# Attention over 16 heads: in every fourth step the row exponentials are kept, turned in 32x32 blocks and multiplied with V in 32x32 tiles

## The chip, the cores and the metric

The kernel runs on one core of one Trainium2 chip. The metric is the time of one execution on the device, in microseconds (us); the median of several runs is compared. All work is in fp32, save the row maxima, which are split into bf16 parts.

## The reference

```python
Q = split_heads(x @ Wq.T + bq); K = split_heads(x @ Wk.T + bk); V = split_heads(x @ Wv.T + bv)
tQ = split_heads(tokens @ Wq.T + bq); tK = split_heads(tokens @ Wk.T + bk)
cQ = Q + tQ;  cK = K + tK
scores = einsum('bhqd,bhkd->bhqk', cQ, cK) / sqrt(32)
out = einsum('bhqk,bhkd->bhqd', softmax(scores), V)
return x + merge_heads(out)
```

Here x is 8 batches of 512 rows and 512 features, there are 16 heads of 32 features, and tokens is one condition vector of 512 features for each batch.

## The kernel before

A **step** t is one batch and four heads (128 features), so there are 32 steps, four to a batch. One core does everything; the program's order on each engine is written out by hand, and PSUM's eight banks are dealt out by a table of turns, `TURNS`, read through `banks(i)`: in each item of a step four banks take scores and four take row scores, and banks that are free again take projections or results.

Each step has four **items**, and in each of them TensorE does the following for other steps than its own as well.

- `exponentials(t, kc)`: the scores of step t **a second time**, keys on the partitions and all 512 queries along the free axis. First a bf16 product with ones (L597) puts the negative row maximum into the bank, then the fp32 product of K and Q (L600) adds the scores. ScalarE (ACT) makes the exponential into a tile `e` (L611).
- `row_max(t+1, qc)`: the scores of the next step, queries on the partitions (`row_scores`, L526). VectorE (DVE) takes the negative maximum over the keys (L494 for one head, L535 for two).
- `denominators(t+1, qc)`: ACT makes the exponential of these row scores with the maximum as its bias (L545). Before, only the sum over the keys is kept (`accum_out`); the exponentials go to a tile `dead` that nobody reads.
- In three items a quarter of the projections of the next batch (q, k, v), done by a scheme of seven block products (`product`, L407): `first_products` and `other_products` in turn, each with additions on DVE (L432, L442, L451, L452, L465, L466).
- In one item (the second) `weighted(t-1)`: 16 products of V with the exponentials (`times_v`, L616), a small product that spreads the sums (`spread_sums`, L647), and `send`: DVE turns the result in 32x32 blocks (L672), POOL multiplies with the reciprocal and adds x and the bias (L673, L674), SP stores it.

Between these, `split_max` (POOL, L559 to L562) and `turn_max` (a transposing DMA on SP's queue) bring the row maxima of the next step into the form that L597 needs; `turn_x` (DVE, L323) turns the next batch's x; `combine_x` (DVE, L333 to L337) makes block sums of it; `load_residual` loads x for the residual and POOL adds the bias (L173).

An fp32 matmul of the code runs as two weight loads and two matmuls, and the profile counts each of them: 512 calls of L526 are 1,024 records.

Of the kernel before, what the change touches and what calls it, by code (L numbers as in the profile page):

```python
# [9 lines left out]
F32 = mybir.dt.float32  # L10
# [7 lines left out]
def kernel(  # L18
# [38 lines left out]
    nc = tc.nc  # L57
# [11 lines left out]
    HS = S // 2  # L69

    const = ctx.enter_context(tc.tile_pool(name="const", bufs=1))
    stage = ctx.enter_context(tc.tile_pool(name="stage", bufs=3))
    xp = ctx.enter_context(tc.tile_pool(name="xp", bufs=4))
    xtp = ctx.enter_context(tc.tile_pool(name="xtp", bufs=2))
    qkp = ctx.enter_context(tc.tile_pool(name="qkp", bufs=3))
    ep = ctx.enter_context(tc.tile_pool(name="ep", bufs=13))
    op = ctx.enter_context(tc.tile_pool(name="op", bufs=2))
# [31 lines left out]
    ]  # L109
    turn = [0]  # L110

    def banks(i, n=1):

        j = TURNS[turn[0]][i]
        if n == 1:
            return psum[:, j, :]
        k = TURNS[turn[0]][i + 1]
        return psum[:, j : k + 1 : k - j, :]

    def advance():  # L120
        turn[0] = {7: 0, len(TURNS) - 1: 4}.get(turn[0], turn[0] + 1)

# [9 lines left out]
    def load_x(n, queue=nc.sync):  # L132

        if n < B * NS:
            xs[n] = xp.tile([P, D], F32, tag="x", name=f"x_{n}")
            queue.dma_start(xs[n], x[n // NS, n % NS * P : (n % NS + 1) * P, :])
# [15 lines left out]

    xr = {}

    def turned_by_vector(t):
# [3 lines left out]
    def load_residual(t):  # L159

        b, g = divmod(t, G)
        if turned_by_vector(t):
            xr[t] = op.tile([P, NB, BL], F32, tag="xr", name=f"xr_{t}", bufs=3)
            for h in range(HG):
                nc.sync.dma_start(
                    xr[t][h * BL : (h + 1) * BL], spread(x[b], g * P + h * BL)
                )
            bias = bvs[:, g, :].unsqueeze(1).broadcast_to([P, NB, BL])
        else:

            xr[t] = xT[b][:, g, :]
            bias = bvl.broadcast_to([P, S])
        nc.gpsimd.tensor_tensor(xr[t], xr[t], bias, ALU.add)  # L173

    ws = {}
    for n in ("q", "k", "v"):
# [21 lines left out]
    load_x(1)  # L198
    wk0 = op.tile([P, D], F32, tag="dead", name="wk0")
    nc.scalar.dma_start(wk0, Wk[:P, :])  # L200

    cond_sb = const.tile([B + 2, D], F32, tag="cond", name="cond_sb")
    nc.sync.dma_start(cond_sb[:B, :], cond)
# [31 lines left out]
    make_identity(nc, ident)  # L235
    split = []
    for i in range(2):
        m = const.tile([P, NS, HG, HD], BF16, tag=f"split{i}", name=f"split{i}")
        nc.vector.memset(m, 0.0)
        split.append(m)  # L240

# [61 lines left out]
    def transpose_x(n, pt, leaves=nc.vector.tensor_copy):  # L303
# [10 lines left out]
        leaves(xT[b][:, :, sc * P : (sc + 1) * P], pt.rearrange("p (c s) -> p c s", c=NC))  # L314
        load_block(n + NC)

    def turn_x(n):
        b, cc = divmod(n, NC)
        if b >= B:
            return  # L320
        if cc == 0:
            xT[b] = xtp.tile([P, NC, S], F32, tag="xT", name=f"xT_{b}")
        nc.vector.transpose(xT[b][:, cc, :], xs[n].rearrange("p f i -> p (f i)"))  # L323
        load_block(n + NC)

# [108 lines left out]
    def first_products(n, b, u, dens, small, at, first=0, held=None):  # L434
# [18 lines left out]
        plus(n, b, u, 1, c22, one_[:, HS:], c12)  # L453

    def other_products(n, b, u, dens, small, at):

# [40 lines left out]

    def row_max(t, qc, hold=False):

# [3 lines left out]
        for j in range(HG):  # L503
            row_scores(t, qc, j, banks(HG + j))
        if t < T - 2 or t * NS + qc == T * NS - 1:
            for j in range(2):
                one_max(t, qc, j, banks(HG + j))
        else:
            row_max_of(t, qc, 0, banks(HG, 2))
        last, both = [banks(HG + 2), banks(HG + 3)], banks(HG + 2, 2)  # L510

        def held():
            if hold and t < T - 2:
                for j in range(2):
                    one_max(t, qc, 2 + j, last[j])
            else:
                row_max_of(t, qc, 1, both)
# [20 lines left out]

    def denominators(t, qc, prs=range(NP)):

        if t >= T - 2:
            return
        for j in [pr * 2 + i for pr in prs for i in range(2)]:
            dead = op.tile([P, S], F32, tag="dead", name=f"dead_{t}_{qc}_{j}")
            nc.scalar.activation(  # L545
                dead,
                banks(HG + j),
                AF.Exp,
# [4 lines left out]
    def split_max(t, on=nc.gpsimd):  # L553

        if t >= T:
            return
# [9 lines left out]
    def turn_max(t):  # L566

        if t >= T:
            return
# [22 lines left out]
    def exponentials(t, kc, at=None):  # L592

        bank = [psum[:, i, :] for i in at] if at else [banks(i) for i in range(HG)]
        for j in range(HG):
# [28 lines left out]
    def times_ones(of, pt, start, stop):  # L624
        for j in range(HG):
# [6 lines left out]
            )  # L632

    def masked(t):

        apart = op.tile([P, HG, NS, NS], F32, tag="apart", name=f"apart_{t}")
        nc.gpsimd.tensor_tensor(
# [7 lines left out]
    def spread_sums(apart, pd):  # L645
        for h in range(HG):
# [6 lines left out]
            )  # L653

    def weighted(t, pt, pd, between):

# [3 lines left out]
        for kc in range(NS):  # L660
            times_v(t, kc, pt)
            if kc == 0:
                spread_sums(apart, pd)
        rec = op.tile([P, NB, 1], F32, tag="recs", name=f"recs_{t}")
        nc.vector.reciprocal(rec, pd[:, :NB].unsqueeze(2))
        between()
        send(t, pt, rec)

    def send(t, y_, rec):

        y = op.tile([P, NB, BL], F32, tag="res", name=f"res_{t}")
        nc.vector.transpose(y.rearrange("p f e -> p (f e)"), y_)  # L672
        nc.gpsimd.tensor_tensor(y, y, rec.broadcast_to([P, NB, BL]), ALU.mult)  # L673
# [16 lines left out]
    def condition(n, pt):  # L690


        for cc in range(NC):
            nc.tensor.matmul(pt[cc * HD : (cc + 1) * HD, :], condT[:, cc, :], wT[n][:, cc, :])  # L694
        part[n] = const.tile([P, D], F32, tag=f"part{n}", name=f"part_{n}")
        nc.scalar.copy(part[n], pt)
# [18 lines left out]
    for _ in range(28):  # L715
        nc.tensor.matmul(warm[:, :P], onesb, onesb, start=True, stop=True)
    def bank(i):
        return psum[:, i, :]

# [84 lines left out]
    parts = {}  # L804

    def part_of(t, pt, of, between=None):

# [4 lines left out]
        if t in parts:  # L812
            p = op.tile([P, S], F32, tag="dead", name=f"part_{t}_{of[0]}")
            nc.scalar.copy(p, pt)
# [17 lines left out]

    for t in range(T - 3):
        b, r = divmod(t, G)

        exponentials(t, 0)
        held = row_max(t + 1, 1, r % 2)
        of = ((t - 1) // G + 1, (t - 1) % G)
        dens = lambda: denominators(t + 1, 1)
        if t:  # L840
            project_pair("q", *of, dens, nothing, 1 if r % 2 else (0, 3), held)
        else:
            first_products("v", 0, 0, dens, nothing, 1)
            turn_x(NC + 2)
            load_residual(1)
        turn_x(t + NC + 3)
        advance()

        exponentials(t, 1)
        row_max(t + 1, 2)  # L850
        dens = lambda: denominators(t + 1, 2)
        if t:
            dens()
            weighted(
                t - 1, banks(0), banks(1), lambda: combine_x(b + 1, r) if r < 2 else None
            )
        else:
            dens()
            other_products("v", 0, 0, nothing, nothing, (0, 2))
        advance()  # L860

        exponentials(t, 2)
        rest = row_max(t + 1, 3, r % 2)

        def held():
            rest()
            split_max(t + 1)
            turn_max(t + 1)

        dens = lambda: denominators(t + 1, 3)  # L870
        if t:
            project_pair("k", *of, dens, nothing, 1 if r % 2 else (0, 3), held)
        else:
            held()
            first_products("v", 0, 1, dens, nothing, 1)
            combine_x(1, 0)
        if t:
            load_residual(t + 1)
        advance()

        exponentials(t, 3)
        held = row_max(t + 2, 0, r % 2)
        dens = lambda: denominators(t + 2, 0)
        project_pair("v", *of, dens, nothing, 1 if r % 2 else (0, 2), held)
        advance()


# [15 lines left out]
    def crossed(t, kc, qc, u=None):  # L903
# [37 lines left out]
        row_max_of(u, qc, 1, banks(HG + 2, 2))  # L941

    t = T - 3
    row(4)
# [59 lines left out]
    sum_of(t, acc2, 2, nc.vector)  # L1004
    den = op.tile([P, NB, BL], F32, tag="dead", name=f"den_{t - 1}")
    nc.vector.transpose(den.rearrange("p f e -> p (f e)"), pd)
# [21 lines left out]

    part_x = op.tile([P, S], F32, tag="dead", name="part_x")
    nc.vector.tensor_tensor(part_x, pd, xr[t], ALU.mult)  # L1030
    den = op.tile([P, S], F32, tag="dead", name="den")
    nc.scalar.copy(den, pd)
    store_30(nc.scalar, (2,))
    oT = op.tile([P, S], F32, tag="res_last", name="oT", bufs=1)
    y = op.tile([P, NS, P], F32, tag="xr_last", name="res", bufs=1)
    rec = op.tile([P, NS, HG, 1], F32, tag="rec", name="rec")
# [57 lines left out]
```

## Time and profile before

| | |
|---|---|
| median of 3 runs (lowest, highest) | 715.58 us (715.08, 716.7) |
| the profiled execution: its time, its span | 717.11 us, 715.0 us |
| granted TensorE clock, mean | 0.998 |
| POOL busy | 176.5 us |
| second scores' exponentials, L611 on ACT | 488 of 603 ns |
| row exponentials, L545 on ACT | 480 of 706 ns, and 225 ns to read each sum |
| a transpose of 128x512 on DVE, L323 | 28 of 701 ns |
| a reduce of 128x512, of 128x1024 on DVE, L494 and L535 | 324 of 685 ns, 88 of 1,215 ns |

The span is the time from the first to the last instruction that the profiler records; the run's own time is some 2 us longer. "Busy" is the union of an engine's recorded instructions; a mean duration can be longer than the distance between two starts, since instructions of an engine overlap. TensorE's matmul ends are modelled. PE is TensorE's matmuls, PEld its weight loads.

### The profile page before, as it was taken

The numbers are of one execution on the slowest core, as the hardware profiler recorded it, in microseconds if no ns is written. First come the engines' busy times: TensorE is split into PE (matmuls) and PEld (weight loads), VectorE is DVE, ScalarE is ACT, GpSimd is POOL, SyncE is SP. The second block draws the span as 40 slices with busy tenths as digits, with TensorE's granted clock in tenths as the row PEclk, the third lists the DMA queues.
The fourth block names the chain that finished last, engine by engine and source line by source line (L and its number), as shares of the span: only waits on it lengthen the run. The fifth ranks groups of instructions, "written<-read, shape, count | busy, mean of one in ns | idle before, by whom it ended". The sixth has DMA issues, their size and how long they took to land.

```text
span 715.0 us, 22748 instructions
## 1 busy us (share of the span) xinstructions
PE 705.7 (99%) x9160; PEld 321.1 (45%) x9160; DVE 535.3 (75%) x918; ACT 604.7 (85%) x1497; POOL 176.5 (25%) x275
## 2 busy tenths in 40 slices
PE   8999999999999999999999999999999999999996
PEld 7445444444444444444444444444444444444431
DVE  4798767877768877778777877777777777667776
ACT  2589888888889899898888889899898898889674
POOL 3712221122221122221122221122221122221451
PEclk9999999999999999999999999999999999999999
DMA  7634321323322323321323321322211222311111
GB/s 181 106 61 68 54 40 29 53 42 51 53 33 41 51 42 50 54 42 32 50 42 52 53 40 32 51 43 49 39 28 17 35 39 39 39 30 19 31 31 30
DMA packets 223390, 33.43 MB, mean 47 GB/s; under 512 B 221610, under 2 KB 222122, under 8 KB 223284
## 3 DMA queue, kind: packets, MB, share of 16 engines
q1 hardware_dynamic: 221524, 30.92, 26.4%
q8 instruction: 72, 1.18, 0.7%
q10 hardware_dynamic: 1760, 1.05, 0.5%
q14 instruction: 34, 0.28, 0.1%
HBM read 19.75 MB, written 8.39 MB: 39 GB/s over the span
## 4 chain that ended last, share of the span: by engine, by line
PE 93%; DVE 2%; DMA 2%; issue 1%; ACT 1%; POOL 0%; SPq 0%; DVEq 0%; POOLq 0%
PE psum L407 39%; PE psum L526 16%; PE psum L616 15%; PE psum L600 14%; PE psum L597 5%; PE psum L350 2%; DMA maxT<-split 1%; DVE acc L894 1%; PE psum L920 1%; DMA w_q<-in_L_cond_Wq_dram 1%; PE psum L266 0%; DVE nmax L535 0%; DVE acc L892 0%; PE psum L694 0%; PE psum L311 0%
## 5 line engine op out<-in xcount | busy, mean ns | idle before, releaser
L545 ACT ACTIVATE dead<-psum,nmax 128x512 f32<-128x512 f32 x480 | 327.4, 706 | 5.6 <-DVE nmax L494 3.1
L611 ACT ACTIVATE e<-psum 128x512 f32<-128x512 f32 x488 | 252.0, 603 | 69.5 <-PE psum L600 69.3
L494 DVE TENSOR_REDUCE nmax<-psum 128x1 f32<-128x512 f32 x324 | 208.3, 685 | 133.4 <-PE psum L526 133.4
L526 PE MATMUL psum<-kT,qT 32*128 32x512 f32 x1024 | 141.1, 598 | 0.0
L673 POOL TENSOR_TENSOR res<-res,recs 128x512 f32<-128x512 f32 x30 | 31.4, 1047 | 419.9 <-DVE res L672 419.9
L600 PE MATMUL psum<-qT,kT 32*128 32x512 f32 x976 | 125.5, 587 | 0.0
L616 PE MATMUL psum<-e,v 128*32 128x512 f32 x1024 | 121.2, 596 | 0.0
L535 DVE TENSOR_REDUCE nmax<-psum 128x2 f32<-128x1024 f32 x88 | 106.8, 1215 | 2.7 <-PE psum L526 2.7
L545 ACT ACTIVATION_READ_ACCUMULATOR dead<-psum,nmax 128x1 f32 x480 | 107.8, 225 | 0.0
L526 PEld LDWEIGHTS psum<-kT,qT 32*128 32x128 f32 x1024 | 59.5, 182 | 55.9 <-ACT dead L545 16.9
L616 PEld LDWEIGHTS psum<-e,v 128*32 128x32 f32 x1024 | 26.6, 110 | 65.1 <-issue 37.6
L407 PE MATMUL psum<-wc_v,xc 128*32 128x256 f32 x768 | 50.2, 379 | 0.0
L600 PEld LDWEIGHTS psum<-qT,kT 32*128 32x128 f32 x976 | 48.6, 185 | 2.2
L597 PE MATMUL psum<-maxT,onesb 3*128 3x512 bf16 x488 | 48.1, 385 | 1.2 <-DMA maxT<-split 1.1
L407 PE MATMUL psum<-xc,wc_k 128*32 128x256 f32 x720 | 47.1, 379 | 0.0
L407 PE MATMUL psum<-xc,wc_q 128*32 128x256 f32 x720 | 47.1, 379 | 0.0
L173 POOL TENSOR_TENSOR xr<-xr,bvs 128x512 f32<-128x512 f32 x31 | 39.4, 1270 | 20.5 <-DMA x<-in_x_dram 13.1
L597 PEld LDWEIGHTS <-onesb 3*128 3x128 bf16 x488 | 12.3, 91 | 65.7 <-issue 60.2
L674 POOL TENSOR_TENSOR res<-res,xr 128x512 f32<-128x512 f32 x30 | 38.6, 1286 | 2.3
L407 PE MATMUL psum<-wT_v,xT 128*32 128x256 f32 x512 | 36.8, 382 | 0.0
L407 PE MATMUL psum<-xT,wT_k 128*32 128x256 f32 x480 | 34.5, 382 | 0.0
L407 PE MATMUL psum<-xT,wT_q 128*32 128x256 f32 x480 | 34.5, 382 | 0.0
(168 smaller groups left out, 710.0 us busy)
## 6 DMA issues: line engine op xcount, KB each, us to landing
xr<-in_x_dram SPq DMA_DIRECT2D x124, 64.0 KB, 2.4
out_dram<-res SPq DMA_DIRECT2D x122, 64.0 KB, 1.9
x<-in_x_dram SPq DMA_DIRECT2D x112, 64.0 KB, 2.4
w_q<-in_L_cond_Wq_dram SPq DMA_DIRECT2D x4, 256.0 KB, 4.2
w_v<-in_L_cond_Wv_dram SPq DMA_DIRECT2D x16, 64.0 KB, 2.3
w_k<-in_L_cond_Wk_dram SPq DMA_DIRECT2D x16, 48.0 KB, 2.4
x<-in_x_dram ACTq DMA_DIRECT2D x2, 256.0 KB, 4.2
x<-in_x_dram SPq DMA_DIRECT2D x2, 256.0 KB, 4.2
```

The costliest lines, as they stand in the source:

```text
L173: nc.gpsimd.tensor_tensor(xr[t], xr[t], bias, ALU.add)
L407: nc.tensor.matmul(pt[r], still[:, r], moving, start=(kc == kcs[0]), stop=(kc == kcs[-1]))
L494: nc.vector.tensor_reduce(nmax[t][:, qc, j : j + 1, 0], pt, AX.X, ALU.max, negate=True)
L526: nc.tensor.matmul(pt, qkT["q", t][r, qc * P : (qc + 1) * P], qkT["k", t][r, :], start=True, stop=True,)
L535: nc.vector.tensor_reduce(nmax[t][:, qc, pr * 2 : pr * 2 + 2, 0], pt, AX.X, ALU.max, negate=True)
L545: nc.scalar.activation(dead, banks(HG + j), AF.Exp, bias=nmax[t][:, qc, j, :], accum_out=sums[t][:, qc, j, :],)
L597: nc.tensor.matmul(bank[j], onesb[r, :], maxT[t][r, :], start=True, stop=False)
L600: nc.tensor.matmul(bank[j], qkT["k", t][r, kc * P : (kc + 1) * P], qkT["q", t][r, :], start=False, stop=True,)
L611: nc.scalar.activation(e[:, i, :], bank[pr * 2 + i], AF.Exp)
L616: nc.tensor.matmul(pt[j * HD : (j + 1) * HD, :], vs[b % 2][:, kc, (g * HG + j) * HD : (g * HG + j + 1) * HD], es[t, kc, j // 2][:, j % 2, ...
L673: nc.gpsimd.tensor_tensor(y, y, rec.broadcast_to([P, NB, BL]), ALU.mult)
L674: nc.gpsimd.tensor_tensor(y, y, xr.pop(t), ALU.add)
```

## The change

It makes seven steps **blocked**: 3, 7, 11, 15, 19, 23 and 27, the last step of each batch but the last.

- For a blocked step, `denominators` writes the row exponentials into a large tile `blocked[t]` (32 KB a partition) instead of `dead`. For all other steps it now writes them over the row scores in PSUM; the tile `dead` is gone.
- A blocked step has no `exponentials`, no `split_max`, no `turn_max`. `turn_blocks` has DVE turn `blocked[t]` in place, in 32x32 blocks: eight operations of 128x1024, five of them in the step before and three in the blocked step (the table `TURNED`).
- `times_blocks` multiplies with V in tiles of 32 rows by 32 columns: 256 calls of 128 columns each, in the order of 16 tiles. After the turn a block of exponentials has its keys on 32 of the partitions, so V is wanted at three rotations by 32 partitions; `move_v` makes these with six DMAs from SBUF to SBUF, in the last item of the step before.
- The result lies in four banks; `send` turns it in four pieces.
- The items are in another order: V, q, k, v in a plain step (v, q, k, v after a blocked one), and q, k, V, B in a blocked one, where B is `times_blocks`. Which bank takes what is now computed (`begin`, `released`).
- In blocked steps the first block products are added by ACT and POOL (`first_by_others`) instead of DVE. `combine_x` is done by POOL. `turn_x` comes two at a time in the first two steps of a batch.
- To make room: three tiles for x instead of four, ten for `e` instead of thirteen, two for the residual instead of three, one for `split` instead of two; tiles of the beginning and the end lie in the large one's place (`early`, `late`).

```diff
+    BLOCKED = [t for t in range(3, T - 4, G)]
-    xp = ctx.enter_context(tc.tile_pool(name="xp", bufs=4))
+    xp = ctx.enter_context(tc.tile_pool(name="xp", bufs=3))
-    ep = ctx.enter_context(tc.tile_pool(name="ep", bufs=13))
+    ep = ctx.enter_context(tc.tile_pool(name="ep", bufs=10))
...
+    def begin(w):
+        rows = order[w : w + 4]
+        pairs = [(j, j + 1) for j in rows if j + 1 in rows]
+        last = max(pairs, key=lambda p: rows.index(p[0]) + rows.index(p[1]), default=sorted(rows[2:]))
+        order[w : w + 4] = [j for j in rows if j not in last] + list(last)
+        row_of[0] = list(order)
+    def released(*roles):
+        order[:] = [row_of[0][i] for i in roles]
...
+    def first_by_others(n, b, u, dens, small, at):
...
+        m1 = c2[:, 0, :]
+        nc.scalar.copy(m1, one_[:, :HS])
...
+            nc.scalar.copy(c1, halves(two_))
+            add = tok[:, "qk".index(n), u * 2 + 1, b : b + 1]
+            nc.scalar.activation(c22, one_[:, HS:], AF.Identity, bias=add)
+        for o in (c1[:, 0, :], c12):
+            nc.gpsimd.tensor_tensor(o, o, m1, ALU.add)
+        nc.gpsimd.tensor_tensor(c22, c22, c12, ALU.add)
...
+    def turn_blocks(t, units):
+        for n in units:
+            e = blocked[t][:, n // NP, n % NP * 2 : n % NP * 2 + 2, :].rearrange("p h s -> p (h s)")
+            nc.vector.transpose(e, e)
+    def move_v(t):
+        b, g = divmod(t, G)
+        m = [ep.tile([P, 2, NS, P], F32, tag="e", name=f"moved_{t}_{i}") for i in range(2)]
+        moved[t] = [m[0][:, 0], m[0][:, 1], m[1][:, 0]]
+        for i in range(1, HG):
+            at = (HG - i) * HD
+            for to, of in ((slice(0, at), slice(i * HD, P)), (slice(at, P), slice(0, i * HD))):
+                nc.sync.dma_start(moved[t][i - 1][to], vs[b % 2][of, :, g * P : (g + 1) * P])
+    def times_blocks(t, pts):
+        b, g = divmod(t, G)
+        whole = vs[b % 2][:, :, g * P : (g + 1) * P]
+        parts = [whole] + moved[t]
+        for i in range(HG):
+            for kc in range(NS):
+                for h in range(HG):
+                    for a in range(HG):
+                        r = slice(a * HD, (a + 1) * HD)
+                        f = kc * HG + (a + i) % HG
+                        nc.tensor.matmul(
+                            pts[a][h * HD : (h + 1) * HD, :P],
+                            parts[i][r, kc, h * HD : (h + 1) * HD],
+                            blocked[t][r, :, h, f * BL : (f + 1) * BL],
+                            start=(i == 0 and kc == 0),
+                            stop=(i == HG - 1 and kc == NS - 1),
+                        )
...
-            dead = op.tile([P, S], F32, tag="dead", name=f"dead_{t}_{qc}_{j}")
+            if t in BLOCKED:
+                to = blocked[t][:, qc, j, :]
+            else:
+                to = banks(w + j)
             nc.scalar.activation(
-                dead,
-                banks(HG + j),
+                to,
+                banks(w + j),
                 AF.Exp,
...
+        if t in BLOCKED:
+            for a in range(HG):
+                nc.vector.transpose(y.rearrange("p (c a) e -> p a c e", a=HG)[:, a], y_[a][:, :P])
+        else:
+            nc.vector.transpose(y.rearrange("p f e -> p (f e)"), y_)
...
+    for t in range(1, T - 3):
         b, r = divmod(t, G)
+        blocks = t in BLOCKED
+        items = ["q", "k", "V", "B"] if blocks else ["v" if t - 1 in BLOCKED else "V", "q", "k", "v"]
+        for i, item in enumerate(items):
+            rows = (t + 1, i + 1) if i < 3 else (t + 2, 0)
+            w = 0 if blocks else HG
+            begin(w)
+            if not blocks:
+                exponentials(t, i)
+            back = i == 0 and not blocks
+            late_first = not blocks and item in "qkv" and (t - 1 - back) % 2 == 0
+            hold = row_max(*rows, late_first, w)
...
+            if item == "B":
+                pts = [banks(4 + a) for a in range(HG)]
+                times_blocks(t, pts)
+                send(t, pts, rec_of_blocks)
+                released(0, 1, 2, 3, 4, 5, 6, 7)
...
+            if i == 3:
+                load_residual(t + 1)
+                if t + 1 in BLOCKED:
+                    move_v(t + 1)
+            turn_more(t, i, 1)
```

## The prediction

> **What bounds the kernel now.** I read the page's busy line first, then the chain that ended last, then that chain piece by piece in a steady stretch, then the engines' busy time by item.
>
> ```profile
> PE 705.7 (99%) x9160; PEld 321.1 (45%) x9160; DVE 535.3 (75%) x918; ACT 604.7 (85%) x1497; POOL 176.5 (25%) x275
> PE 93%; DVE 2%; DMA 2%; issue 1%; ACT 1%; POOL 0%; SPq 0%; DVEq 0%; POOLq 0%
> ```
>
> TensorE (PE) is busy 99% and carries 93% of the chain. "Busy" alone would not prove it, since matmuls overlap; the chain in order of time does (start, us, line and records):
>
> ```profile
> 302.52 0.33 PE psum L597 x4
> 302.85 0.86 PE psum L600 x8
> 303.71 0.86 PE psum L526 x8
> 304.57 3.16 PE psum L407 x56
> ...
> 309.80 0.99 PE psum L616 x8
> 310.79 0.05 PE psum L647 x7
> 310.84 2.59 PE psum L616 x24
> ```
>
> Each piece begins where the one before ended: no gap, no other engine. (An fp32 matmul of the code is two records, so 4 calls show as x8.) A step is four items. Each holds second scores (L597 0.33, L600 0.86) and row scores (L526 0.86); three add a projection (3.16), one the product with V (3.58 and 0.05). That is 4 x 2.05 + 3 x 3.16 + 3.63 = 21.3 us. Busy time in the four items of one step:
>
> ```profile
> 276.70:282.00 5.30, 5.30 (x80) 2.66 (x78) 3.95 (x6) 4.84 (x12) 1.12 (x2) 1.00 0.79 81
> 282.00:287.30 5.30, 5.30 (x80) 2.80 (x78) 4.11 (x9) 4.73 (x12) 0.00 (x0) 1.00 0.02 4
> 287.30:292.70 5.40, 5.40 (x64) 1.73 (x61) 3.54 (x6) 4.82 (x12) 0.00 (x0) 1.00 0.31 49
> 292.70:298.05 5.35, 5.35 (x84) 2.54 (x76) 4.00 (x9) 4.73 (x12) 3.20 (x6) 1.00 0.11 20
> ```
>
> After the stretch and its length come PE, PEld, DVE, ACT and POOL. PE fills 21.35 us of 21.35; ACT has 19.1, DVE 15.6, POOL 4.3. So PE's work is what counts, as long as ACT and DVE stay below it. The clock column is 1.00 throughout.
>
> **The change, part by part.** Seven steps are blocked (3, 7, ... 27).
>
> *Removed from PE in a blocked step.* The second scores, 4 x (0.33 + 0.86) = 4.76, and the product with V in its old form, 0.99 + 2.59 = 3.58: 8.34 us, all on the path. ACT also loses 16 exponentials (L611, 603 ns each, about 0.52 apart, 8.3 us), which lay under PE.
>
> *Added to PE: `times_blocks`.* It makes 256 calls, 512 records of 32 rows by 32 columns and 128 moving columns, over 16 tiles, 32 records to a tile. No row of the trace has this form, so I bound it.
>
> By data: a projection runs 56 records of 256 columns over 4 tiles in 3.16 us, 14 to a tile, 0.226 us each; 128 columns are 0.113, and 32 of them 3.6 us, if all 16 tiles run at once. By issue, the quickest row is the small product of the denominators:
>
> ```profile
> 310.61 0.23 PE L647 MATMUL psum<-apart,modulo 128*32 128x16 f32 x8
> 310.67 1.04 PE L616 MATMUL psum<-e,v 128*32 128x512 f32 x8
> ```
>
> Eight records begin within 0.06 us before the next group; the chain gives 7 in 0.05, 7.1 ns each, and 512 at that pace are 3.7 us. This is only a short run over four tiles. The slow end is the quickest pace that lasts: 56 records in 3.16 us, 56.4 ns each, or 28.9 us for 512. There the data set the pace (256 columns on four tiles), so the true pace can hardly be that bad, but no row excludes it. Then instructions must arrive:
>
> ```profile
> q8 instruction: 72, 1.18, 0.7%
> ```
>
> 72 loads for PE's 18,320 records are 254 records a load, and 0.7% of 16 x 715 us over 72 is 1.1 us a load. `times_blocks` is 1,024 records with their weight loads, four loads, 4.4 us if they come one after another. I take 4.4, next to the two rows at 3.6 and 3.7, and keep 3.6 and 28.9 as ends.
>
> The Trainium skill speaks against the change here: "TensorE: Matmul & The Clock Gate", section "Wait — 56ns, not 53.3ns?", says that matmuls never start less than about 25 ns apart, however small. As an estimate from that page, 512 of them would be 12.8 us, and the kernel about 750 us; the eight L647 records above began some 7 ns apart, so the rule does not hold for a short run over several tiles, and no row shows a long one. Another page pulls the other way: "Runtime: NRT & Kernel Launch", section "Instruction fetch mechanics", says that instruction refills are mostly hidden; by it the loads would add nothing, and the sum would be near 686.
>
> *The turns on VectorE.* Eight in-place transposes of 128x1024, which the trace lacks. The 128x512 one (L323) is 701 ns, a reduce of 128x1024 (L535) 1,215 ns: between 1.2 and 1.4 us, I take 1.22, since operations of 512 elements cost 0.68 to 0.70 and those of 1024 cost 1.22, whatever they do. Five lie in the step before, three in the blocked one. The step shown has 15.6 us of DVE with one L323 in it; the step before a blocked one loses that and gains five turns: 15.6 - 0.7 + 6.1 = 21.0 of 21.3. They fit, barely. In the blocked step: 15.6 - 0.7 + 3.7, less two first products moved to ACT and POOL (2 x 1.72 from L442, L451, L452, L432), plus 0.5 for the result turned in four pieces: 15.7, against PE's 21.3 - 8.34 + 4.4 = 17.4. If this cover were gone, each turn would cost its 1.22.
>
> *A new wait.* The result of `times_blocks` lies in four banks, and the next step's row scores need them. Its four small turns cost 0.25 (L665) to 0.42 us (L452's 128x256) each, so up to 1.7 us after the last matmul, while PE has 1.19 us of second scores to do meanwhile: 0 to 0.5 us of stall. I take 0.5. What queues behind the waiting row score on PE is that item's projection.
>
> *Denominators written into PSUM in place* (25 steps; into SBUF in the blocked ones). No row has ACT writing PSUM. The nearest, L545 and L611, write SBUF at 706 and 603 ns. A saving would lie under PE, worth nothing; I take no cost. If writing in the bank that is read doubled the 0.66 us between starts, an item's ACT would be 4.8 + 4 x 0.66 = 7.4 of 5.3 us: see the rivals.
>
> *Moves at nothing.* Both halves of `combine_x` to POOL (four at 1.27 a batch; POOL is busy 25%). The copies of the moved first products on ACT, about 1.4 an item, where the second exponentials' 2.07 went. `move_v`'s six DMAs on SP's queue, about 0.55 us of issue each, a step ahead of their use; behind them there wait only the next loads and stores, and the transposing DMA of the row maxima comes two items later. Fewer buffers (3 for x, 10 for e, one `split`): the loads land in 2.4 us and are asked for steps ahead; `weighted` now runs in the first item, so 8 + 2 tiles of e are live. The maxima's path (L559 to the DMA, about 6 us in the trace) has 3.63 + 0.86 + 4.4 = 8.9 us to hide in before the step that follows a blocked one, and 3.16 + 2.05 + 3.16 = 8.4 elsewhere, as now.
>
> *Sum.* -8.34 + 4.4 + 0.5 = -3.4 us a blocked step, x 7 = -24 us. The profiled execution took 717.1 us (span 715.0 and 2.1 around it), so 693 there; the median of the runs, 715.58, is 1.5 lower: 692.
>
> **Rivals.**
>
> *VectorE sets the pace.* For it: 21.0 of 21.3 us in the step before, with a row maximum waiting behind each turn. Against: the sum still fits, and ACT follows with some slack (4.8 of 5.3). At 1.4 us a turn that step has 21.9; with 1.5 us lost there and 1 in the blocked step, 2.5 x 7 = 17 us of the gain go: 709, still faster.
>
> *`times_blocks` is paced by issue* (slower). One mechanism: PE cannot be handed 1,024 short records as fast as 16 tiles could eat them. It decides from (8.34 - 0.5) / 512 = 15.3 ns a record. For it: no row shows a long run under 56 ns. Against: the burst at 7 ns, and that the slow rows are explained by their data. At the geometric middle of 7.1 and 56.4, 20 ns, it takes 10.2 us, +2.4 a step, 732; at 56.4, 28.9 us and about 863.
>
> *ACT is slower in place in PSUM.* At the doubled end, 2.1 us an item x 100 items, some 925 us; against it stands only that nothing suggests it.
>
> *The change does nothing*: the saved and added PE time cancel (`times_blocks` at 7.8 us): within 0.2%.
>
> **How the numbers follow.** Forecast 0.55 (682 to 700: `times_blocks` of 3.6 without stall is -33, of 5.5 with it -16); VectorE 0.17; issue-paced 0.23; PSUM 0.03; cancelled 0.02. A measurement of this kernel can tell about 0.2% from no change. So faster 0.72, same 0.02, slower 0.26. The range must take in the VectorE case and the issue-paced one to 20 ns (732, and 3 for the ends' rounding): 682 to 735; beyond lie the worse half of the issue-paced case and the PSUM one. The forecast's own range, since both signs have weight, is 682 to 700.
>
> **What would show it.** Right: the 32x32 group has 3,584 records, and its stretches last 4 to 5 us; the blocked step is near 18 us and the three others 21.3; PE still without gaps. Issue-paced: the stretches last over 8 us with PE's records evenly apart. VectorE: PE gaps before L526 released by ACT behind DVE in the step ahead. Wrong outright: ACT's denominators longer than 0.7 us in the 25 other steps, or gaps at L597 after a blocked step that wait for the transposing DMA.

## The result, and the profile after

The kernel with the change takes 760.8 us (median of 4 runs, 759.63 to 762.04), against 715.79 for the kernel before beside it: a ratio of 1.0628, 95% interval 1.0607 to 1.0649. It is 45 us slower, 6.4 us for each of the seven blocked steps, where 692 us had been forecast. The profiled execution took 760.85 us (span 759.1). Line numbers move: L597, L600, L526, L407, L616 and L647 of before are L694, L697, L579, L435, L713 and L748 now; `times_blocks` is L623, `turn_blocks` L598.

First the busy line, the shares of the chain, and the row of instruction loads, the same three places of the page as before:

```profile
PE 717.0 (94%) x12184; PEld 351.5 (46%) x12184; DVE 562.9 (74%) x899; ACT 562.4 (74%) x1427; POOL 233.6 (31%) x315
PE 94%; issue 5%; DVE 1%; DMA 0%; DVEq 0%
q8 instruction: 95, 1.56, 0.9%
```

TensorE (PE) was busy 99% and is 94% now; "issue", time in which an engine waits for nothing that the profile shows, has gone from 1% to 5% of a longer chain. There are 23 more instruction loads. The chain in order of time shows where, from the last items of step 15 on (start, us, line and records):

```profile
302.23 1.07 PE psum L579 x8
303.30 0.99 PE psum L713 x8
304.29 0.05 PE psum L748 x7
304.35 2.59 PE psum L713 x24
306.94 1.46 PE psum L579 x8
308.40 2.47 PE psum L623 x135
310.87 1.37 issue
312.24 1.89 PE psum L623 x95
314.12 2.12 issue
316.24 2.58 PE psum L623 x127
318.82 1.43 issue
320.24 2.07 PE psum L623 x84
322.32 0.55 PE psum L694 x4
322.86 1.24 PE psum L697 x6
```

`times_blocks` lasts 13.9 us here, not 4.4, and holds three holes. Busy time by item and by piece of that stretch (after the stretch and its length come PE, PEld, DVE, ACT, POOL, and after these the granted clock, DMA share and GB/s):

```profile
293.71:297.94 4.23, 4.23 (x68) 2.03 (x68) 4.23 (x7) 2.25 (x8) 0.00 (x0) 1.00 0.01 2
297.94:302.23 4.29, 4.29 (x76) 2.09 (x76) 4.29 (x7) 4.19 (x12) 1.83 (x3) 1.00 0.01 4
302.23:306.94 4.71, 4.71 (x52) 1.32 (x51) 4.12 (x6) 4.70 (x14) 2.92 (x7) 1.00 0.00 0
306.94:322.32 15.38, 10.47 (x524) 7.66 (x528) 3.20 (x5) 3.18 (x10) 2.84 (x4) 0.82 0.27 47
...
312.24:314.12 1.88, 1.88 (x128) 1.54 (x128) 0.00 (x0) 0.00 (x0) 0.00 (x0) 1.00 0.65 109
314.12:316.24 2.12, 0.01 (x1) 0.00 (x1) 0.00 (x0) 0.00 (x0) 0.00 (x0) 1.00 0.36 54
316.24:318.82 2.58, 2.58 (x128) 1.92 (x128) 0.00 (x0) 0.00 (x0) 0.00 (x0) 0.58 0.25 42
318.82:320.24 1.42, 0.00 (x0) 0.00 (x0) 0.00 (x0) 0.00 (x0) 0.00 (x0) 0.50 0.00 0
320.24:322.32 2.08, 2.08 (x89) 1.54 (x93) 0.00 (x0) 0.00 (x0) 0.00 (x0) 0.50 0.03 8
322.32:324.96 2.64, 2.64 (x24) 1.04 (x28) 0.91 (x4) 0.83 (x2) 1.43 (x2) 0.78 0.00 0
```

Two things are to be seen. From 312.24 to 320.24 us DVE, ACT and POOL do nothing: nobody computes what PE might be waiting for. And each piece between two holes has exactly 128 matmul records and 128 weight loads, 256 instructions. In all seven blocked steps the holes lie 128 records apart (after records 171, 299 and 427 in this one; 144, 272, 400 in the first), and a stretch lasts 12.1 to 13.8 us from its first to its last start, 12.93 on average. The row of loads gives 256 as well: 95 loads for 24,368 PE instructions. In this stretch the records of that queue have loads at 309.82, 313.34, 317.81 and 321.37 us, of 0.95 to 1.57 us; each begins 0.9 to 1.6 us after PE has gone into a new load's instructions (at record 43, by the count of 128, and behind each hole), and PE goes on 1.3 to 1.5 us after its end. So the cycle is 4.0 us here (312.24, 316.24, 320.24) while PE works off 256 instructions in 1.9. Over the seven stretches the distance from one hole's end to the next is 3.45 to 4.02 us, 3.8 on average.

The clock column is a second loss. After two holes it falls to 0.5, and is still low in the next item: L697 there takes 1.24 us instead of 0.86. In this execution the clock fell in four of the seven stretches.

The groups answer the other steps of the sum:

```profile
L642 ACT ACTIVATE psum<-psum,nmax 128x512 f32<-128x512 f32 x368 | 245.9, 681 | 31.1 <-DVE nmax L546 26.8
L623 PE MATMUL psum<-blocks,moved 32*32 32x128 f32 x2688 | 47.1, 304 | 35.3 <-issue 35.3
L598 DVE STREAM_TRANSPOSE blocks<-blocks 128x1024 f32<-128x1024 f32 x56 | 67.8, 1210 | 0.0
```

The turns take 1.21 us. In-place exponentials in PSUM take 681 ns, less than the 706 of before into SBUF. The L623 row has idle time ahead of it that is put down to "issue" alone (the quarter that reads V itself is a group of its own).

### The profile page after: what moved, and what is told of

Its sections match the earlier page's. It is cut to its first block, busy times and chain, and to the rows that moved or that the text cites. A ratio compares the mean times of both kernels' runs of the same rounds, so it can differ in the third digit from the quotient of the medians.

```text
span 759.1 us, 28405 instructions
## 1 busy us (share of the span) xinstructions
PE 717.0 (94%) x12184; PEld 351.5 (46%) x12184; DVE 562.9 (74%) x899; ACT 562.4 (74%) x1427; POOL 233.6 (31%) x315
## 4 chain that ended last, share of the span: by engine, by line
PE 94%; issue 5%; DVE 1%; DMA 0%; DVEq 0%
PE psum L435 38%; PE psum L579 16%; PE psum L713 12%; PE psum L697 11%; PE psum L623 8%; PE psum L694 4%; PE psum L378 2%; PE psum L1094 1%; DMA w_q<-in_L_cond_Wq_dram 0%; PE psum L723 0%; PE psum L293 0%; PE psum L338 0%; PE psum L803 0%; PE psum L748 0%; PE psum L790 0%
## 5 line engine op out<-in xcount | busy, mean ns | idle before, releaser
L708 ACT ACTIVATE e<-psum 128x512 f32<-128x512 f32 x376 | 194.2, 602 | 131.4 <-PE psum L697 128.0
L642 ACT ACTIVATE psum<-psum,nmax 128x512 f32<-128x512 f32 x368 | 245.9, 681 | 31.1 <-DVE nmax L546 26.8
L546 DVE TENSOR_REDUCE nmax<-psum 128x1 f32<-128x512 f32 x298 | 190.9, 682 | 82.0 <-PE psum L579 80.7
L579 PE MATMUL psum<-kT,qT 32*128 32x512 f32 x1024 | 147.6, 610 | 0.0
L697 PE MATMUL psum<-qT,kT 32*128 32x512 f32 x752 | 98.9, 600 | 0.0
L713 PE MATMUL psum<-e,v 128*32 128x512 f32 x800 | 95.3, 597 | 0.0
L579 PEld LDWEIGHTS psum<-kT,qT 32*128 32x128 f32 x1024 | 60.2, 184 | 59.3 <-issue 20.6
L642 ACT ACTIVATION_READ_ACCUMULATOR psum<-psum,nmax 128x1 f32 x368 | 81.9, 223 | 0.0
L623 PE MATMUL psum<-blocks,moved 32*32 32x128 f32 x2688 | 47.1, 304 | 35.3 <-issue 35.3
L642 ACT ACTIVATE blocks<-psum,nmax 128x512 f32<-128x512 f32 x112 | 76.2, 719 | 0.0
L598 DVE STREAM_TRANSPOSE blocks<-blocks 128x1024 f32<-128x1024 f32 x56 | 67.8, 1210 | 0.0
L623 PEld LDWEIGHTS psum<-blocks,moved 32*32 32x32 f32 x2688 | 36.1, 108 | 43.6 <-issue 41.4
L435 PE MATMUL psum<-wc_v,xc 128*32 128x256 f32 x768 | 50.2, 379 | 0.0
L435 PE MATMUL psum<-xc,wc_q 128*32 128x256 f32 x720 | 47.1, 379 | 0.0
L435 PE MATMUL psum<-xc,wc_k 128*32 128x256 f32 x720 | 47.1, 379 | 0.0
L713 PEld LDWEIGHTS psum<-e,v 128*32 128x32 f32 x800 | 20.8, 110 | 51.4 <-issue 29.2
L697 PEld LDWEIGHTS psum<-qT,kT 32*128 32x128 f32 x752 | 38.4, 191 | 1.9
```

Of the source, the lines that this page charges most:

```text
L435: nc.tensor.matmul(pt[r], still[:, r], moving, start=(kc == kcs[0]), stop=(kc == kcs[-1]))
L546: nc.vector.tensor_reduce(nmax[t][:, qc, j : j + 1, 0], pt, AX.X, ALU.max, negate=True)
L579: nc.tensor.matmul(pt, qkT["q", t][r, qc * P : (qc + 1) * P], qkT["k", t][r, :], start=True, stop=True,)
L598: nc.vector.transpose(e, e)
L623: nc.tensor.matmul(pts[a][h * HD : (h + 1) * HD, :P], parts[i][r, kc, h * HD : (h + 1) * HD], blocked[t][r, :, h, f * BL : (f + 1) * BL], ...
L642: nc.scalar.activation(to, banks(w + j), AF.Exp, bias=nmax[t][:, qc, j, :], accum_out=sums[t][:, qc, j, :],)
```

## Experiments

The theory, formed on the trace: *arrival*. PE's instructions come in loads of 256; PE has the load that it is in and the next one, and a further one is asked for only as it goes into a new load, with some 4.0 us (3.45 to 4.02) until it can be used. Work with more than some 64 instructions a microsecond (256 in 4.0 us) runs dry. The rivals: *data* (128 moving columns on 16 tiles), *pace* (PE starts such records no quicker), and that *the rest of the change* costs the time.

**None blocked.** All of the change but its subject:

```diff
-    BLOCKED = [t for t in range(3, T - 4, G)]
+    BLOCKED = []
```

> The changed kernel with no blocked step: all else of the change stays (the order of the items, the computed banks, denominators written over the scores in PSUM, combine_x on POOL, the smaller pools). If the loss of 45 us lies in the blocked steps alone, 713 to 719 us. If the rest of the change costs something (ACT slower in place in PSUM, fewer buffers, POOL), over 725 us, and then the seven blocked steps cost less than 6.4 us each.

Measured: 725.7 us, ratio 1.0127 (1.0103 to 1.0151); by the time alone that is the second outcome, but the trace puts the loss elsewhere. The first row scores of step 28 begin at 619.4 us, before at 619.7: with POOL's `combine_x`, the PSUM in place, fewer buffers and the new banks' order, the steady steps are as they were. The 10 us lie in the last six distances from one set of row scores to the next, 31.4 us together instead of 20.9, with PE waiting there for DVE's maxima. Probably the banks come to the end in another order when no step is blocked (this is argued, not shown); the changed kernel has 20.8 there. So the 45 us belong to the blocked steps, with what only they have (the turns, `move_v`, `first_by_others`).

**One round in sixteen.** Only 16 of the 256 calls:

```diff
-        for i in range(HG):
-            for kc in range(NS):
+        for i in range(1):
+            for kc in range(1):
```

> times_blocks makes only its first round, 16 of its 256 calls (32 of 512 records); the product with V is left out for the rest, all other work of the change stays. This is the sum without its disputed term: 8.34 us saved in a blocked step, less about 0.3 for the 32 records and 0.5 to 1 of stall, 715.8 - 7 x 7.3 = 665 us. If VectorE or ACT held the blocked steps, 690 or more.

Measured: 704.34 us, ratio 0.9829 (0.9805 to 0.9854). The 32 records take 0.24 us, 7.5 ns apart, and the step should have gained 7 us. It gained 1.75. The chain shows why (below it, a line of the waits of the whole run: us in total, times, longest):

```profile
290.68 1.46 PE psum L579 x8
292.14 0.75 PE psum L623 x32
...
292.97 1.23 DVE nmax L588
...
294.81 0.87 ACT psum L642 x3
295.68 0.04 issue
295.72 0.58 PE psum L694
296.30 1.71 PE psum L697 x8
...
PE psum L694 <- DMA maxT<-split: 12.8, 7, 2.9
```

The next scores need the banks of the row scores just made, and these are free only when DVE has their maxima and ACT its four exponentials: 3.6 us after L579's end PE may go on, and then at half the clock (1.71 instead of 0.86). A second way bears on it: in each of the seven steps L694 first waits for the transposing DMA that brings the row maxima (1.2 to 2.9 us, 12.8 together), and for the banks behind it (3.3 us together). In five of the steps the banks come last, as in this one; in two L694 waits for the DMA alone, 2.7 and 2.9 us. These two ways bound the step when `times_blocks` is as short as this.

**A quarter of the columns.** The calls with 32 moving columns instead of 128:

```diff
-                            pts[a][h * HD : (h + 1) * HD, :P],
+                            pts[a][h * HD : (h + 1) * HD, :BL],
...
-                            blocked[t][r, :, h, f * BL : (f + 1) * BL],
+                            blocked[t][r, 0, h, f * BL : (f + 1) * BL],
```

> times_blocks keeps its 512 records but moves 32 columns instead of 128 in each (a quarter of the queries; the others' results are left out). Arrival theory (PE's instructions come in loads of 256, one in 4.0 us, and times_blocks needs four): unchanged, 755 to 763 us, gaps after the same numbers of records. Data theory (16 tiles eat 128 columns no faster): the stretch shrinks from 12.9 us to 4 or 5, about 700 us. Pace theory (PE starts no record sooner than some 17 ns after the last): unchanged too.

Measured: 763.51 us, ratio 1.065 (1.0633 to 1.0668), no gain, and the holes lie after the same records (144, 272, 400 in the first step). Between two holes of step 15, 128 records now begin within 1.1 us instead of 1.6, and the hole behind them is longer by as much, 2.7 us instead of 2.1. So the columns count between the holes, but not for the length of the stretch: the data are out.

**Filled.** Three fp32 products of 384 columns after each of the first three quarters, into columns that nobody reads:

```diff
+            if i < HG - 1:
+                for _ in range(3):
+                    nc.tensor.matmul(
+                        pts[0][:, P:], ident, wT["q"][:, 0, P:], start=False, stop=True, skip_group_check=True
+                    )
```

> After each of the first three quarters of times_blocks three extra fp32 matmuls of 128x128 by 384 columns, into columns that nobody reads: six records of 0.32 us, 1.9 us of PE work each time, 5.8 us in a blocked step, 40 us in all, with 36 instructions. Arrival theory: the gaps of 1.6 to 2.4 us are filled, and the time stays at 755 to 770 us. Pace or data theory (PE itself is the limit): about 800 us.

Measured: 764.16 us, ratio 1.0665 (1.0649 to 1.068). The chain, with the filler at L632:

```profile
309.87 1.83 PE psum L623 x102
311.70 2.13 PE psum L632 x6
313.83 1.83 PE psum L623 x102
315.67 2.27 PE psum L632 x6
317.94 1.78 PE psum L623 x99
```

21 pieces of filler of at least 2.1 us, some 45 us of work, cost 3.4 us (2.6 against the kernel before beside each): most of it lies in the holes, and PE's idle time before L623 that is put down to "issue" falls from 35.3 us in all to 1.2. The clock stays at 0.999. A limit on the pace of the short records would have added the filler to them.

**Half and three quarters of the calls.** Two kernels, with 512 and 768 instructions:

```diff
-        for i in range(HG):
+        for i in range(2):    # range(3) in the other
```

> Only the first two of the four rotations are multiplied, 128 of the 256 calls of a blocked step (half of the V product is left out): 256 records, 512 instructions. Theory of arrival (each 256 instructions of PE are one load, and a load's cycle is about 4.0 us when PE outruns it, with one load or a little more held ahead): one or two gaps instead of three, a stretch of 5 to 6.5 us instead of 12 to 14, so some 7 us less in each of seven steps: 761 - 49 = 712 (706 to 718). Theory of a gap that belongs to the ends (the stretch pays 6 us of gaps once, whatever its length): stretch of 9 to 10 us, 735. In both, what the run with 16 calls showed (704) is a floor: there the next row scores wait for their banks anyway.

> Three of the four rotations, 192 of the 256 calls (a quarter of the V product is left out): 384 records, 768 instructions, between the run with half of the calls (704.9, stretch about 5.0 us, one gap) and the changed kernel (760.8, about 12.9 us, three gaps). Theory of arrival: one gap more than with half, at the same record numbers as in the changed kernel (171 and 299 in the step that has 171, 299, 427 there); stretch about 9.1 us, so seven times 4.1 more than with half: 733 (728 to 738). If instead something grows faster than the number of loads, it stays below 720 or lies near 760.

Measured: 704.89 us, ratio 0.9844 (0.9829 to 0.9859), with one hole after the very records of before (171 in the step shown) and stretches of 4.4 to 5.2 us; and 734.69 us, ratio 1.0267 (1.025 to 1.0284), two holes, stretches of 8.4 to 9.5 us. From 512 instructions to 768 and to 1,024 the stretch grows by 4.0 us each time (4.95, 8.90, 12.93). The half gained some 7 us more than arrival alone said (712), and no more than 16 calls had. Its stretch covers both ways of that run (L694 follows it without a wait in all seven steps) and the clock falls in one step only, where with 16 calls PE waits 3.6 us and then runs at half the clock.

**Half floats.** The exponentials that are kept and V as float16 in blocked steps, so that a call is one weight load and one matmul instead of two and two:

```diff
-                    blocked[t] = room(f"blocks_{t}")
+                    half = room(f"blocks_{t}").rearrange("p c h s -> p (c h s)")[:, : NS * HG * S // 2]
+                    blocked[t] = half.bitcast(F16).rearrange("p (c h s) -> p c h s", c=NS, h=HG)
...
-        m = [ep.tile([P, 2, NS, P], F32, tag="e", name=f"moved_{t}_{i}") for i in range(2)]
-        moved[t] = [m[0][:, 0], m[0][:, 1], m[1][:, 0]]
+        m = ep.tile([P, HG, NS, P // 2], F32, tag="e", name=f"moved_{t}").bitcast(F16)
+        moved[t] = [m[:, i] for i in range(HG)]
+        nc.gpsimd.tensor_copy(m[:, 0], vs[b % 2][:, :, g * P : (g + 1) * P])
```

> All 256 calls, but the kept exponentials and V as float16 in blocked steps (their precision is reduced there): one weight load and one matmul for each call, so again 512 instructions, and 256 records of one pass. ACT writes float16, VectorE turns 16-bit blocks, POOL casts V, the moves on SP's queue carry half the bytes. Theory of arrival by number of instructions: the same stretch as the run with half of the calls, 5 to 6.5 us, and 706 to 718 us, perhaps a little less as turns or moves of 16-bit data are cheaper. If instead calls cost (about 53 ns each in the changed kernel, 13.6 us for 256), it stays near 761. If the turns are what holds the step, and they are quicker in 16 bits, it falls below the run with 16 calls (704).

Measured: 706.73 us, ratio 0.9873 (0.9846 to 0.99). With the full product, though at a lower precision, it is faster than both kernels, by 9 and 54 us. The chain, with the lines one or two further on (L624 is `times_blocks`), has one hole:

```profile
292.46 1.46 PE psum L580 x8
293.92 1.69 PE psum L624 x171
295.61 2.49 issue
298.10 0.91 PE psum L624 x85
299.01 0.33 PE psum L696 x4
```

The turns cost the same in 16 bits (1,210 ns), so they are not what was gained. But besides the instructions the passes and the bytes have halved too; the next run parts these.

**Half floats, calls cut in two.** Each call as two of 64 columns: the same data, 1,024 instructions again.

```diff
+                        for c in range(2):
                             nc.tensor.matmul(
-                            pts[a][h * HD : (h + 1) * HD, :P],
+                                pts[a][h * HD : (h + 1) * HD, c * P // 2 : (c + 1) * P // 2],
                                 parts[i][r, kc, h * HD : (h + 1) * HD],
-                            blocked[t][r, :, h, f * BL : (f + 1) * BL],
+                                blocked[t][r, 2 * c : 2 * c + 2, h, f * BL : (f + 1) * BL],
```

> The float16 version with each call cut in two of 64 columns: the same data, the same arithmetic, but 512 weight loads and 512 matmuls, 1,024 instructions as in the changed kernel. Theory of arrival by number of instructions: the gain of float16 goes again, three gaps, stretch of 12 to 14 us, 755 to 765. If fp32's passes (or the bytes of the moving data) had set the stretch, it stays near the float16 version with whole calls (706.7), at most 7 x 3 us above it.

Measured: 764.85 us, ratio 1.0679 (1.066 to 1.0699). The same step has its three holes back, after the same records 171, 299 and 427:

```profile
310.81 1.67 PE psum L625 x95
312.48 1.82 issue
314.29 1.42 PE psum L625 x83
315.71 2.86 issue
318.57 1.42 PE psum L625 x79
319.99 2.31 issue
```

The data, their type and the arithmetic are the same at 706.7 and at 764.9 us; each call has become two, with twice the weight loads and matmuls.

**Half floats around the scores.** The last row scores between the halves of `times_blocks`, to fill the hole that is left:

```diff
+            if item == "B":
+                pts = [banks(4 + a) for a in range(HG)]
+                times_blocks(t, pts, range(2))
             hold = row_max(*rows, late_first, w)
...
-                pts = [banks(4 + a) for a in range(HG)]
-                times_blocks(t, pts)
+                times_blocks(t, pts, range(2, HG))
```

> The float16 version with the row scores of the last item set between the two halves of times_blocks instead of ahead of them: the same work, but 16 slower instructions (0.9 to 1.5 us) stand near the one gap that is left (2.0 to 2.8 us). Theory A, the load alone holds that step: the scores fill part of the gap, and a step gains about 1 us: 700 (697 to 703). Theory B, the way of the banks holds it as well (row scores, VectorE's maxima, ACT's four exponentials, some 4.5 us from the last score until the next step's scores may begin, as in the run with 16 calls): the scores now come 2 us later and what the gap gives the banks take, and the first half also waits for the bank of the product with V: 705 to 716, not faster than the float16 version (706.7). I expect B.

Measured: 719.25 us, ratio 1.004 (1.0025 to 1.0055). It lost 12 us, a little more than either theory allowed:

```profile
293.38 1.07 PE psum L580 x8
294.45 0.49 PE psum L624 x43
294.94 0.82 issue
295.75 1.14 DVE nmax L589
...
296.92 1.46 ACT psum L644 x4
...
299.00 1.71 PE psum L699 x8
```

The hole shrinks from 2.0 to 2.8 us to 1.1 to 1.7 (from start to start), but the banks come later: PE waits for DVE and ACT behind the scores, as with 16 calls, and goes on at half the clock (L699 takes 1.71). The first half also waits up to 0.7 us for the bank of the product with V, as theory B had it. So with half floats neither order is free: the hole bounds the one, the banks the other.

**One sum for all.** A blocked step loses 8.34 us of old work and gains the stretch. Its four row scores cost 1.07, 1.07, 1.07 and 1.46 us instead of 0.86, 1.23 more. (The run with the scores between the halves has no place in the table, since they lie in its stretch.) So the change of a step should be the stretch less 7.11:

| run | PE instructions | stretch, mean us | less 7.11 | measured (time - before) / 7 | clock |
|---|---|---|---|---|---|
| 16 calls | 64 | 0.24 | -6.9 | -1.7 | 0.978 |
| half floats | 512 | 4.65 | -2.5 | -1.3 | 0.994 |
| half of the calls | 512 | 4.95 | -2.2 | -1.6 | 0.996 |
| three quarters | 768 | 8.90 | +1.8 | +2.7 | 0.992 |
| the change | 1,024 | 12.93 | +5.8 | +6.4 | 0.983 |
| half floats, cut | 1,024 | 12.20 | +5.1 | +7.0 | 0.947 |
| a quarter of the columns | 1,024 | 12.09 | +5.0 | +6.7 | 0.948 |
| filled | 1,024 + 36 | 13.87 | +6.8 | +6.8 | 0.999 |

In the one run whose clock is whole the sum holds to 0.1 us; elsewhere 0.6 to 1.9 us come on top, most in the two runs with the lowest clock. With the half floats they lie in the first item of the next step: from its row scores to the following ones it takes 6.46 us on average, the next one 5.20. The clock is low in two of these steps; the rest is not explained. With 16 calls the banks and the transposing DMA, and the clock that falls behind them, add 5 us. To break even, the stretch must stay under some 6 to 6.5 us (7.11 less those 0.6 to 1.2); at 3.45 to 4.0 us a load, no run with 1,024 instructions came near it (11.7 us at the least).

## Why the prediction was wrong, by its steps

- **The step that failed: `times_blocks` at 4.4 us; it measured 12.93.** The sum had seen that four loads would come, and took them at 1.1 us each "if they come one after another". That was the time of the transfer only. The transfer was right (0.95 to 1.57 us), but 2.4 to 3 us of each cycle lie around it: a load begins 0.9 to 1.6 us after PE enters the one before, and PE goes on 1.3 to 1.5 us after its landing. The trace of before did not show it: a load lasted 9.9 us there (715 us over 72), so the cycle of 4.0 never came to light. The bounds of 3.6 and 28.9 held it.
- **The quick pace.** 7 ns a record is right for the first 32 records of a stretch (7.5 ns with 16 calls alone). Behind them it is not: a piece of 128 records takes 1.88 us, 1.62 from its first start to its last, which is 12.8 ns each. Without holes `times_blocks` would still be an estimated 6.5 us by this, about the break-even.
- **The removed 8.34 us** are gone, but the row scores that the second scores used to precede became 1.23 us longer a step. L579 takes mostly 0.86 behind the second scores, a product of its own form, but 1.07 in all 26 places where a projection (L435, L378) runs ahead of it, and 1.46 behind the product with V. This was no term of the sum, though the trace of before had it: L526 takes 1.07 in the five places where no second scores run ahead of it.
- **The stall of 0.5 us.** The banks of the result cost nothing that the chain shows, and with a stretch of 4.65 us (half floats) L696, the next scores' first product, follows without a wait. It is at 0.24 us that the banks of the row scores and the transposing DMA hold PE, 3.6 us after the row scores in step 15, and the clock then halves. The prediction's 8.9 us for the maxima's path counted on the 4.4 of `times_blocks`; its sign of gaps behind that DMA came true in that run. Even with `times_blocks` about as short as predicted the time was about 706 (half floats, 4.65 us), not 692: the 1.23 of the row scores, and the 1.2 in the next step that are in part unexplained, were missing in the sum.
- **Right:** the turns (1.22 predicted, 1.21 measured); the step before fits (DVE 21.0 us predicted, 19.6 of 21.4 measured in its four items, PE without a hole); DVE in the blocked step (15.7 predicted, 15.8 in the four windows above); PSUM in place (681 ns); the moves at nothing (none blocked: the steady steps unchanged with `combine_x` on POOL and fewer buffers; `move_v`: in the changed kernel `times_blocks` waits for "issue" alone).
- **The rivals.** VectorE did not set the pace. The issue-paced rival had the right sign and a chance of 0.23, and its break-even of 15.3 ns a record is passed (25.3 on average), but its mechanism is not what the trace shows: it wanted records evenly apart, at 20 ns or so, and 732 us. What it said, that PE cannot be handed so many short records, is true of the loads; PE's own pace, 12.8 ns, is under the break-even. The sign "stretches over 8 us" pointed there, the sign "evenly apart" away. The range to 735 fell short since it stopped at 10.2 us, a middle of two paces that had nothing to do with the cause.

The two rules that were weighed stand thus. "TensorE: Matmul & The Clock Gate" in the Trainium skill, section "Wait — 56ns, not 53.3ns?", gave 12.8 us by a floor of about 25 ns between matmuls, close to what was measured. The agreement is by chance: 32 records began 7.5 ns apart, 128 at 12.8 ns, and 256 in float16 took 4.65 us, 18 ns each, their hole included. "Runtime: NRT & Kernel Launch", section "Instruction fetch mechanics", says that loads are of 256 instructions, that the next is fetched while the current one is executed, and that crossing is mostly hidden. The first two agree with the holes 128 records apart and with the loads' begins; the third agrees with 254 instructions in 9.9 us, where PE was busy 99%, and not with 256 in 1.9.

## What to carry to other kernels

Count the instructions of a stretch, not only its cycles: here PE was fed 256 instructions in 3.45 to 4.0 us, 64 to 74 a microsecond, and an fp32 call is four of them, so 256 calls of 32x32 tiles took 12.1 to 13.8 us, and 11.7 to 12.9 with a quarter of the data. When such a stretch must be, halve its instructions (one pass instead of two was worth 54 us here). Long matmuls between them ran almost for nothing, but those were useless ones; the one try with useful work, the row scores, lost 12 us to the banks. And ask of each shortened stretch what it used to hide: at 0.24 us the ways of the row scores, over VectorE and ScalarE to free banks and over the transposing DMA, set the step; at 4.65 us PE no longer waited for them.

A whole blocked step has about 1,390 PE instructions (1,024, two projections with 112 each, four row scores with 16 each, some 80 for the product with V). At 3.45 to 4.0 us for 256 that is an estimated 18.8 to 21.7 us against the old step's 21.4: with fp32, spreading the calls over the step would gain less than 3 us a step, perhaps nothing. This was not tried.

## What the runs showed of the hardware

- In the runs with 512 to 1,024 short PE instructions on end, in fp32 and float16, with 32, 64 or 128 columns, PE stopped after 256 at a time (for the first time 288 to 496 instructions into the stretch): holes of 0.7 to 2.9 us put down to "issue". In the changed kernel there are 3.45 to 4.02 us from one hole's end to the next.
- The granted clock answers to the holes: in step 15 it fell in the third piece, after two holes of 1.4 and 2.1 us, stayed at 0.5 until the stretch ended, and rose again within the 2.6 us behind it (0.78 there). It fell in four of the seven stretches of the changed kernel (0.983 over the span). With the holes filled by matmuls it fell in none (0.999); with 32-column or cut calls, which leave PE idle longer, it fell in all seven (0.948 and 0.947).
- 32 records on 16 tiles begin within 0.24 us, but a piece of 128 of them goes at 12.8 ns each on average: the short run is no measure for the long one.
